# Adds in front of the exponential, and a maximum moved past dense products, in a two-layer transformer kernel

## The chip, the cores and the metric

The kernel runs on one core of one Trainium2 chip. Five engines of the core matter: TensorE multiplies matrices (PE in the profile, PEld for its weight loads), VectorE (DVE), ScalarE (ACT) and GpSimd (POOL) work element by element, and SyncE (SP) issues nearly all DMAs. Each engine takes its own instructions strictly in the order in which they were issued; between engines, semaphores hold an instruction until what it reads is written and what it overwrites is free. The metric is the device time of one execution in microseconds, the median of several runs.

## What is computed

Two layers work on 4 sequences of 1024 tokens with 256 channels. The first layer is a recurrent attention and a mixture of eight experts. The second layer, which holds the change, is an attention over pairs of tokens and a gated feed-forward network with three wide products. The core of the pair attention, per query token i and key token j:

```python
q = einsum('bnc,ac->bna', X, Wq)          # 64 features a
k = einsum('bnc,ac->bna', X, Wk)
e = relu(rho(q[:, :, None, :] + k[:, None, :, :]))   # in effect sqrt(relu(q + k) + eps)
scores = einsum('bija,a->bij', e, Wphi)
m = max(scores, axis=-1)
ex = exp(scores - m)
part1 = einsum('bij,bjc->bic', ex, Vy)
Ew = einsum('bij,bija->bia', ex, e)       # e weighted with ex
out = (part1 + Ew @ We) / sum(ex)
```

The feed-forward network after it is silu(x W1) * (x W2), then two 1024x1024 layers with Gelu, then W3.

## The kernel before

The function `pair_attention` runs the second layer, from 1269 us to the end. It writes out the order of all instructions by hand.

**Blocks, pairs and slots.** There are 128 blocks (class `Block`), each for 32 queries. The 64 features and 32 queries of a block are handled as 16 tiles of 128 partitions x 1024 keys, two to a *pair*, so eight pairs to a block. A pair lives in one buffer `s` of a ring of 14. Its life has four steps:

- `begin` (L1377 ff.) takes a ring buffer and lets POOL do its adds (L1381): the tile number i (0 to 15) in `ADD_ON_POOL`.
- `adds` (L1386) lets VectorE add what neither POOL nor ScalarE has (L1392).
- `pair` (L1396) lets ScalarE add the tiles in `RELU_ON_SCALAR` (L1403), take the square root of the whole pair (L1404), and lets TensorE sum the features into the block's scores `sc` (L1408), eight matmuls that the profile counts as 16.
- `weigh` (L1454), on VectorE, multiplies a tile with the spread exponentials `xb` and sums. After both tiles of a pair the ring buffer is free.

Here an add is relu(key + query), with the query as a per-partition scalar.

**The maximum and the exponential.** When the scores of a block are complete, `top` takes the maximum over a row quarter (L1418), places it in one of four columns (`quarters`, L1420), and a small product with `same` (L1421) brings the four quarters together. `exps` takes the negated maximum (`neg`, L1425, VectorE) and the exponential (`ex`, L1427, ScalarE), and calls `switch`, which runs the dense stream's waiting Silu or Gelu (L1357). The exponential and the root need different activation tables, so a table load stands ahead of each change. `spread` copies the exponentials to all partitions (L1434, TensorE, into `xb`), which the next block's weighings need.

**The main loop** goes over blocks n and slots p = 0 to 7. A slot weighs the two tiles of pair p of block n, with the adds of the pair to be made between them, then issues `work(ROOM[p])`, a counted portion of other work, and then begins one pair and makes one pair that was begun two slots ahead. The pair made in slot p is number 8n + p + 12: pairs 4 to 7 of block n + 1 in slots 0 to 3, pairs 0 to 3 of block n + 2 in slots 4 to 7. So the scores of block n + 1 are complete in slot 3; its maximum comes in slot 5, its exponential in slot 6.

**Other work.** `work` first runs what is due of the dense stream on VectorE (`tick`: the scalings of dense products, L1280 and L1299, two slots after the product), then issues matmuls of the feed-forward network (L1245 for the first products, L1315 for the two wide layers, L1336 for the last) and of the finished blocks (L1505, L1517). One group of dense products takes eight blocks, and it stops at each Silu or Gelu until the next exponential. Lines L913, L922, L926 and L929 are its layer norm.

The places in the loop that the change touches:

```python
cur.weigh(p, 0, ew)
if made < 8 * N:
    blocks[made // 8].adds(made % 8)
cur.weigh(p, 1, ew)
if nxt and p == 5:
    blocks[n + 1].top()
if nxt and p == 6:
    blocks[n + 1].exps()
    blocks[n + 1].spread(0)
work(ROOM[p])
```

Of the kernel before, what the change touches and what calls it, by code (L numbers as in the profile page):

```python
# [8 lines left out]
AF = mybir.ActivationFunctionType  # L9
# [22 lines left out]
PREP = 12  # L32
ROOM = (4, 6, 6, 6, 6, 4, 3, 6)
LATE = 2
RELU_ON_SCALAR = (2, 6, 8, 12, 14)
FIRST_ON_SCALAR = 6
ADD_ON_POOL = (1, 3, 5, 9, 11, 13)
LEAD = 2
# [5 lines left out]
@with_exitstack  # L44
def block_kernel(ctx: ExitStack, tc: tile.TileContext, a, out):
    nc = tc.nc
    keep = ctx.enter_context(tc.tile_pool(name="keep", bufs=1))


    kept = ctx.enter_context(tc.tile_pool(name="kept", bufs=1, space=DRAM))  # L50
    link = {
        "x1": [kept.tile([U, C], F32, tag=f"x1_{j}", name=f"x1_{j}") for j in range(B * T // U)],
        "x2": [kept.tile([FB, C], F32, tag=f"x2_{j}", name=f"x2_{j}") for j in range(B * T // FB)],
        "gates": [kept.tile([1, 2, B, C], F32, tag=f"gates{j}", name=f"gates{j}") for j in range(2)],
        "brow": kept.tile([1, C], F32, tag="brow", name="brow"),
        "yg": kept.tile([P, 4, U], F32, tag="yg", name="yg"),
        "qd": kept.tile([T, 64], F32, tag="qd0", name="qd0"),
        "kd": kept.tile([8, P, T], F32, tag="kd0", name="kd0"),
        "vd": kept.tile([T, C + 1], F32, tag="vd0", name="vd0"),
    }  # L60

    ident = keep.tile([P, P], F32, tag="ident", name="ident")
    nc.scalar.dma_start(ident, a["ident"])
    eps = keep.tile([P, 3], F32, tag="eps", name="eps")
    for i, v in enumerate((EPS_LN, EPS_GN, EPS_RHO)):
        nc.vector.memset(eps[:, i : i + 1], v)
    cols = [keep.tile([P, 6, 2, B], F32, tag=f"mcols{i}", name=f"mcols{i}") for i in range(2)]
    seen = keep.tile([P, NE], F32, tag="seen", name="seen")
    link["qt"] = [keep.tile([P, 64, 8], F32, tag=f"qt{i}", name=f"qt{i}") for i in range(2)]
    nc.gpsimd.memset(seen, 0.0)  # L70
    first_layer(tc, a, link, cols, seen, ident, eps)
    pair_attention(tc, a, link, out, cols, seen, ident, eps)
# [750 lines left out]
def pair_attention(tc, a, link, out, cols_of, seen, ident, eps):  # L823
# [10 lines left out]
    nc = tc.nc  # L834
    NB = T // 32
# [3 lines left out]
    with tc.tile_pool(name="at_k", bufs=1) as pk, tc.tile_pool(name="at_w", bufs=1) as wp, tc.tile_pool(  # L839
# [14 lines left out]
        kB, qtab, kds, vds = {0: {}}, {0: link["qt"][0]}, {0: link["kd"]}, {0: link["vd"]}  # L854
# [18 lines left out]
        for i in range(2):  # L873
            t = wp.tile([P, 4, P], F32, tag=f"ewt{i}", name=f"ewt{i}")
            nc.gpsimd.memset(t, 0.0)
            ewt.append(t)
            t = wp.tile([P, 4, 64], F32, tag=f"ew{i}", name=f"ew{i}")
# [168 lines left out]
        def tick():  # L1046
            for x in late:
                x[0] -= 1
            while late and late[0][0] <= 0:
                late.pop(0)[1]()  # L1050
                banks[0] += 1
# [205 lines left out]
        def follower():  # L1257

            return groups.get(stream[1]) if len(stream) > 1 else None
# [103 lines left out]
        class Block:  # L1363


            def __init__(self, n):
                self.n, self.b, self.s, self.added = n, n // NB, {}, set()
                self.sc = psc.tile([P, 512], F32, tag="sc", name="sc")

            def on_scalar(self, i):  # L1370
                return i in RELU_ON_SCALAR if self.n else i < FIRST_ON_SCALAR

# [3 lines left out]
            def begin(self, p):  # L1376
                self.s[p] = ring.tile([P, 2, T], F32, tag="s", name="s")  # L1377
                for h in range(2):
                    i = 2 * p + h
                    if self.n and i in ADD_ON_POOL:  # L1380
                        nc.gpsimd.tensor_scalar(  # L1381
                            self.s[p][:, h, :], kB[self.b][i % 8], self.query(i), 0.0, ALU.add, ALU.max
                        )

            def adds(self, p):
# [3 lines left out]
                for h in range(2):  # L1389
                    i = 2 * p + h  # L1390
                    if not (self.n and i in ADD_ON_POOL or self.on_scalar(i)):
                        nc.vector.tensor_scalar(  # L1392
                            self.s[p][:, h, :], kB[self.b][i % 8], self.query(i), 0.0, ALU.add, ALU.max
                        )

            def pair(self, p):  # L1396
                t = self.s[p]
                s = p // 4
                self.adds(p)
                for h in range(2):  # L1400
                    i = 2 * p + h
                    if self.on_scalar(i):
                        nc.scalar.activation(t[:, h, :], kB[self.b][i % 8], AF.Relu, bias=self.query(i))  # L1403
                nc.scalar.activation(t, t, AF.Sqrt, bias=eps_rho)  # L1404
                for h in range(2):
                    g = (2 * p + h) % 8
                    for j in range(4):
                        nc.tensor.matmul(  # L1408
                            self.sc[32 * j : 32 * j + 32, 0:256],
                            wsel[:, g, 16 * (1 - s) : 16 * (1 - s) + 32],  # L1410
                            t[:, h, 256 * j : 256 * (j + 1)],
                            start=p == 0 and h == 0,
                            stop=p == 7 and h == 1,
                        )
# [121 lines left out]
        N = B * NB  # L1536
        blocks = {0: Block(0)}
        begun = made = 0
# [3 lines left out]
        def work(room):  # L1542


            tick()
            turns[0] += 1
            if issues and turns[0] % 2:
                issues.pop(0)()
            for of in (tasks, stream):
                while of and room > 0:  # L1550
                    got = next(of[0], self_done)
                    if got is self_done:
                        of.pop(0)
                    elif got is None:
                        break
                    else:
                        room -= got
# [10 lines left out]
        def make():  # L1568
            nonlocal made
            n, p = made // 8, made % 8  # L1570
            if n < N:
                blocks[n].pair(p)
                if n % NB == NB - 1 and n + 1 < N and p >= 4:
                    for g in range(2 * p - 8, 2 * p - 6):
                        spread_keys(n // NB + 1, g)
            made += 1
# [13 lines left out]
        for n in range(N):  # L1590
            cur = blocks.pop(n)
            ew = ews[n // 4 % 2]
            if n % 4 == 0:
                exT = p2.tile([P, 4, 2, P], F32, tag="exT", name="exT")
            nxt = n + 1 < N
            if n % NB == PREP and n // NB + 1 < B:
                stream.insert(min(1 + (follower() in heads), len(stream)), prepare(n // NB + 1))
            for p in range(8):
                if p == 0:
                    cur.spread(1)  # L1600
                    cur.turn()
                if p == 2:
                    cur.turned(exT)
                cur.weigh(p, 0, ew)
                if made < 8 * N:
                    blocks[made // 8].adds(made % 8)
                cur.weigh(p, 1, ew)
                if nxt and p == 5:
                    blocks[n + 1].top()
                if nxt and p == 6:  # L1610
                    blocks[n + 1].exps()
                    blocks[n + 1].spread(0)
                work(ROOM[p])
                while begun <= 8 * n + p + ahead[0]:
                    begin()
                    make()
            if n % 4 == 3:
                tasks.append(finish(n, ew, exT))
# [104 lines left out]
```

## Time and profile before

| what | value |
|---|---|
| median of 3 runs | 5141.64 us (5141.53 to 5143.81) |
| profiled execution | 5137.34 us |
| its span | 5135.6 us, 75609 instructions |
| granted TensorE clock, mean | 0.90 |
| ScalarE roots (L1404) | 1024, 2000 ns each |
| ScalarE adds (L1403) | 641, 1138 ns each |
| VectorE weighings (L1454) | 2048, 1209 ns each |
| VectorE adds (L1392) | 645, 922 ns each |
| POOL adds (L1381) | 762, 3792 ns each |
| exponentials (L1427) | 128, 473 ns each |

A row of a group gives the line of the kernel, the engine, the operation, the tiles written and read, how often, then the busy time and the mean of one, and after the bar the idle time of the engine just before these instructions and which engine's work ended it. A row of a timeline gives start and duration in us. Two instructions that follow each other on VectorE or ScalarE can overlap by about a tenth of a microsecond in such rows, so the distance from start to start is the better price. All times within an execution are counted from the start of its span.

### The profile page before, as it was taken

How to read it: one execution, taken by the hardware profiler on the slowest of the kernel's cores; microseconds unless marked ns; L12 is line 12 of the kernel's file. 1: busy time of each engine (PE TensorE's matmuls, PEld its weight loads, DVE VectorE, ACT ScalarE, POOL GpSimd, SP SyncE). 2: the span in 40 equal slices, each digit the busy share in tenths (PEclk: the TensorE clock that was granted, in tenths of full speed). 3: DMA queues.
4: the chain of work that ended last, by engine and by line, in shares of the span. 5: the costliest groups of instructions: out<-in, count | busy, mean ns of one | idle time of the engine just before them, and what ended most of it. 6: DMA issues, size and time to landing. Idle time of an engine off the chain costs nothing.

```text
span 5135.6 us, 75609 instructions
## 1 busy us (share of the span) xinstructions
PE 4334.1 (84%) x28714; PEld 2437.5 (47%) x28714; DVE 4175.7 (81%) x7255; ACT 3690.1 (72%) x3438; POOL 3396.9 (66%) x1233
## 2 busy tenths in 40 slices
PE   6788888877688979888887988888889889798888
PEld 2233333333234635555554555555455556455557
DVE  5877777765799888888888888888888988988871
ACT  2322222213899889999998889999888999999961
POOL 3533343433688777787887778788867877887840
PEclk8798888988798989999898999999889999999999
DMA  4233333344011222222121323222223222121223
GB/s 137 85 101 105 96 97 89 88 115 117 18 36 58 82 86 87 98 74 83 61 73 51 118 76 111 69 78 71 72 72 108 99 77 80 62 79 66 73 82 114
DMA packets 255787, 429.16 MB, mean 84 GB/s; under 512 B 71752, under 2 KB 142592, under 8 KB 255168
## 3 DMA queue, kind: packets, MB, share of 16 engines
q1 hardware_dynamic: 251776, 420.76, 25.8%
q8 instruction: 227, 3.72, 0.3%
q10 hardware_dynamic: 3168, 1.99, 0.1%
q0 software_dynamic: 480, 1.57, 0.1%
q14 instruction: 136, 1.11, 0.1%
HBM read 396.13 MB, written 40.67 MB: 85 GB/s over the span
## 4 chain that ended last, share of the span: by engine, by line
PE 34%; ACT 18%; DVE 15%; issue 7%; POOL 1%; DMA 0%; ACTq 0%; POOLq 0%; SPq 0%; DVEq 0%
PE ff_ps L1315 14%; PE sc L1408 10%; DVE s L1454 9%; ACT s L1404 9%; ACT s L1403 4%; PE xb L1434 2%; DVE s L1392 2%; PE out_ps L1336 2%; PE o L1505 2%; ACT L1404 2%; ACT L1357 1%; PE o L1517 1%; PE ff_ps L1245 1%; ACT wide L1357 1%; ACT ex L1427 1%
## 5 line engine op out<-in xcount | busy, mean ns | idle before, releaser
L1381 POOL TENSOR_SCALAR s<-kB,qt 128x1024 f32<-128x1024 f32 x762 | 2879.7, 3792 | 603.6 <-DVE ew L1454 480.4
L1454 DVE CUSTOM_DVE_ANT_0 s<-s,xb 128x1024 f32<-128x1024 f32 x2048 | 2417.0, 1209 | 35.1 <-PE xb L1434 33.7
L1404 ACT ACTIVATE s<-s,eps 128x2048 f32<-128x2048 f32 x1024 | 2027.6, 2000 | 76.0 <-DVE s L1392 30.4
L1408 PE MATMUL sc<-s,wsel 128*32 128x256 f32 x16384 | 1198.5, 417 | 404.6 <-ACT s L1404 402.5
L1315 PE MATMUL ff_ps<-wide,fw 128*128 128x256 f32 x4096 | 1006.0, 395 | 29.2 <-ACT wide L1357 25.6
L1408 PEld LDWEIGHTS sc<-s,wsel 128*32 128x32 f32 x16384 | 456.2, 115 | 1006.9 <-ACT s L1404 600.3
L1315 PEld LDWEIGHTS ff_ps<-wide,fw 128*128 128x128 f32 x4096 | 765.7, 194 | 237.6 <-issue 99.5
L1403 ACT ACTIVATE s<-kB,qt 128x1024 f32<-128x1024 f32 x641 | 728.9, 1138 | 23.5 <-DMA yg<-out_g 22.8
L1392 DVE TENSOR_SCALAR s<-kB,qt 128x1024 f32<-128x1024 f32 x645 | 594.1, 922 | 0.4 <-DMA kB<-kd 0.4
L729 POOL TENSOR_TENSOR kv<-vb,out_k 128x512 f32<-128x512 f32 x256 | 323.1, 1270 | 285.5 <-DVE state L797 225.5
L607 PE MATMUL e_ps<-wd,hid 128*128 128x512 f32 x896 | 429.1, 626 | 34.0 <-DVE acc L590 33.2
L1434 PE MATMUL xb<-ex,pick 64*128 64x256 f32 x2048 | 324.9, 440 | 56.9 <-ACT ex L1427 56.9
L797 DVE TENSOR_TENSOR_SCAN state<-dec,carry,kv 128x512 f32<-128x512 f32 x256 | 325.9, 1273 | 9.9 <-POOL carry L792 5.0
L607 PEld LDWEIGHTS e_ps<-wd,hid 128*128 128x128 f32 x896 | 176.0, 202 | 281.0 <-issue 273.4
L1434 PEld LDWEIGHTS xb<-ex,pick 64*128 64x128 f32 x2048 | 195.4, 206 | 194.6 <-ACT ex L1427 96.8
L1245 PE MATMUL ff_ps<-wide,fw 128*128 128x256 f32 x1024 | 266.0, 409 | 6.1 <-ACT wide L929 5.8
L799 DVE TENSOR_TENSOR pr<-state,rec 128x512 f32<-128x512 f32 x256 | 176.0, 687 | 113.2 <-ACT state L795 66.5
L789 ACT COPY carry<-state 128x1 f32<-128x1 f32 x255 | 47.8, 187 | 263.9 <-DVE state L797 262.9
L1245 PEld LDWEIGHTS ff_ps<-wide,fw 128*128 128x128 f32 x1024 | 197.4, 202 | 64.9 <-issue 25.3
L1418 DVE TENSOR_REDUCE sc<-sc 128x1 f32<-128x256 f32 x128 | 54.9, 429 | 208.9 <-PE sc L1408 208.8
L1299 DVE TENSOR_TENSOR wide<-ff_ps,ffn_s 128x512 f32<-128x512 f32 x128 | 87.7, 685 | 167.7 <-PE ff_ps L1315 167.7
L1427 ACT ACTIVATE ex<-sc,neg 128x256 f32<-128x256 f32 x128 | 60.6, 473 | 201.0 <-DVE neg L1425 200.1
(254 smaller groups left out, 4002.8 us busy)
## 6 DMA issues: line engine op xcount, KB each, us to landing
fw<-in_ffw_dram SPq DMA_DIRECT2D x354, 512.0 KB
vb<-vd SPq DMA_DIRECT2D x1024, 64.0 KB
lent<-vd SPq DMA_DIRECT2D x64, 514.0 KB
wd<-in_w_down_dram SPq DMA_DIRECT2D x28, 1024.0 KB
kB<-kd SPq DMA_DIRECT2D x32, 512.0 KB
lent<-in_We_dram SPq DMA_DIRECT2D x32, 512.0 KB
kd<-nd SPq DMA_DIRECT2D x24, 512.0 KB
vd<-out_v SPq DMA_DIRECT2D x8, 512.0 KB
```

The lines of the kernel that those rows point to most:

```text
L607: nc.tensor.matmul(ps, hid[:, k, t * P : (t + 1) * P], wd[:, k, :], start=k == 0, stop=k == HID // P - 1)
L729: nc.gpsimd.tensor_mul(kv, vb[:, g % 2, :], ready[u]["k"][:, n // HN, :])
L797: nc.vector.tensor_tensor_scan(s[:, 1 : U + 1], dec, kv, c, ALU.mult, ALU.add)
L1245: nc.tensor.matmul(ps[:, h, :], w[:, k, o : o + P], hT[:, k, :], start=k == 0, stop=k == 1)
L1315: nc.tensor.matmul(ps[:, h, :], w[:, k * P : (k + 1) * P], of[:, k, :], start=k == 0, stop=k == 7)
L1381: nc.gpsimd.tensor_scalar(self.s[p][:, h, :], kB[self.b][i % 8], self.query(i), 0.0, ALU.add, ALU.max)
L1392: nc.vector.tensor_scalar(self.s[p][:, h, :], kB[self.b][i % 8], self.query(i), 0.0, ALU.add, ALU.max)
L1403: nc.scalar.activation(t[:, h, :], kB[self.b][i % 8], AF.Relu, bias=self.query(i))
L1404: nc.scalar.activation(t, t, AF.Sqrt, bias=eps_rho)
L1408: nc.tensor.matmul(self.sc[32 * j : 32 * j + 32, 0:256], wsel[:, g, 16 * (1 - s) : 16 * (1 - s) + 32], t[:, h, 256 * j : 256 * (j + 1)], s ...
L1434: nc.tensor.matmul(xb[:, 256 * j : 256 * (j + 1)], pick[q, j % 2, s, :], self.ex[q, :], start=True, stop=True)
L1454: nc.vector.tensor_tensor_reduce(t[:, h, :], t[:, h, :], self.xb[s], 1.0, 0.0, ALU.mult, ALU.add, ew[:, self.n % 4, col : col + 1])
```

## The change

Three things are moved; nothing is computed differently. Two of ScalarE's tiles are others (2 and 6 become 4 and 7). In slot 6, ScalarE's adds of the two pairs that are begun and not yet made (pairs 2 and 3 of block n + 2) are issued ahead of the exponential, by a new method `relus` that notes which pairs have had it. In the same slot, `exps` moves from behind the second weighing to between the weighings. In slot 5, `top` moves from ahead of `work` to behind it.

```diff
-RELU_ON_SCALAR = (2, 6, 8, 12, 14)
+RELU_ON_SCALAR = (4, 7, 8, 12, 14)
...
+            def relus(self, p):
+                if p in self.relued:
+                    return
+                self.relued.add(p)
+                for h in range(2):
+                    i = 2 * p + h
+                    if self.on_scalar(i):
+                        nc.scalar.activation(self.s[p][:, h, :], kB[self.b][i % 8], AF.Relu, bias=self.query(i))
+
             def pair(self, p):
                 t = self.s[p]
                 s = p // 4
                 self.adds(p)
-                for h in range(2):
-                    i = 2 * p + h
-                    if self.on_scalar(i):
-                        nc.scalar.activation(t[:, h, :], kB[self.b][i % 8], AF.Relu, bias=self.query(i))
+                self.relus(p)
                 nc.scalar.activation(t, t, AF.Sqrt, bias=eps_rho)
...
                 cur.weigh(p, 0, ew)
                 if made < 8 * N:
                     blocks[made // 8].adds(made % 8)
+                if nxt and p == 6:
+                    for m in range(made, min(begun, 8 * N)):
+                        blocks[m // 8].relus(m % 8)
+                    blocks[n + 1].exps()
                 cur.weigh(p, 1, ew)
+                if nxt and p == 6:
+                    blocks[n + 1].spread(0)
+                work(ROOM[p])
                 if nxt and p == 5:
                     blocks[n + 1].top()
-                if nxt and p == 6:
-                    blocks[n + 1].exps()
-                    blocks[n + 1].spread(0)
-                work(ROOM[p])
```

With these tiles VectorE keeps 0, 2, 6, 10 and 15 instead of 0, 4, 7, 10 and 15; POOL's six are the same.

More of the change, by code (lines that the diff above doesn't have):

```diff
@@ L1366, in __init__ @@
             def __init__(self, n):
-                self.n, self.b, self.s, self.added = n, n // NB, {}, set()
+                self.n, self.b, self.s, self.added, self.relued = n, n // NB, {}, set(), set()
                 self.sc = psc.tile([P, 512], F32, tag="sc", name="sc")
```

## The prediction

> **What bounds the kernel now.** I read the page first, then the last stage (the pair scores, 1269 to 4990 us, 3721 of 5135.6 us), then one repeating stretch of it. Only this stage holds the edited lines.
>
> ```profile
> PE 4334.1 (84%) x28714; PEld 2437.5 (47%) x28714; DVE 4175.7 (81%) x7255; ACT 3690.1 (72%) x3438; POOL 3396.9 (66%) x1233
> ...
> L1418 DVE TENSOR_REDUCE sc<-sc 128x1 f32<-128x256 f32 x128 | 54.9, 429 | 208.9 <-PE sc L1408 208.8
> ...
> L1427 ACT ACTIVATE ex<-sc,neg 128x256 f32<-128x256 f32 x128 | 60.6, 473 | 201.0 <-DVE neg L1425 200.1
> ```
>
> ScalarE waits 200 us at the exponential for the negated maximum, VectorE 209 us at the maximum for TensorE's scores. These are the two places that the change touches.
>
> The starts of the exponential repeat every eight blocks, with the dense products of one group. One such cycle lies between the exponentials at 4229.33 and 4456.71 us: blocks of 31.71, 28.65, 26.33, 29.44, 29.43, 24.71, 30.89 and 26.22 us; I call them A to H. The windows view of it:
>
> ```profile
> 4229.80:4457.20 227.40, 194.83 (x1592) 120.27 (x1584) 200.70 (x357) 208.64 (x156) 184.11 (x52) 0.92 0.20 70
> ```
>
> ScalarE (fourth figure) has 208.6 of 227.4 us to do, VectorE 200.7, TensorE 194.8: none of the three has 15% to spare, and each waits for another in turn. The waits of the same cycle:
>
> ```profile
> ACT ex L1427 <- DVE neg L1425: 11.1, 4, 4.6
> DVE sc L1418 <- PE sc L1408: 9.8, 5, 4.4
> ```
>
> So only four of eight exponentials wait: A 2.07, B 3.95, C 0.47, E 4.64 us. In D, F, G and H ScalarE comes to its exponential after the maximum is there. The timelines of the end of E, of TensorE, then ScalarE, then VectorE (start, duration, idle before):
>
> ```profile
> 4372.36 1.07 PE L1408 MATMUL sc<-s,wsel 128*32 128x256 f32 x16
> 4373.36 0.38 PE L1421 MATMUL sc<-quarters,same 128*128 128x4 f32 x2
> 4373.60 1.97 PE L1315 MATMUL ff_ps<-wide,fw 128*128 128x256 f32 x8
> 4375.50 1.07 PE L1408 MATMUL sc<-s,wsel 128*32 128x256 f32 x16
> 4376.51 1.13 PE L1434 MATMUL xb<-ex,pick 64*128 64x256 f32 x8
> ```
>
> ```profile
> 4368.96 1.28 ACT L1427 ACT_TABLE_LOAD   x1
> 4374.88 0.47 ACT L1427 ACTIVATE ex<-sc,neg 128x256 f32<-128x256 f32 x1 [4.64 <-DVE neg L1425]
> 4375.38 1.28 ACT L1404 ACT_TABLE_LOAD   x1
> ```
>
> ```profile
> 4369.78 0.43 DVE L1418 TENSOR_REDUCE sc<-sc 128x1 f32<-128x256 f32 x1 [2.65 <-PE sc L1408]
> ...
> 4370.92 1.21 DVE L1454 CUSTOM_DVE_ANT_0 s<-s,xb 128x1024 f32<-128x1024 f32 x1
> ...
> 4372.06 1.59 DVE L1392 TENSOR_SCALAR s<-kB,qt 128x1024 f32<-128x1024 f32 x1
> 4373.57 1.20 DVE L1454 CUSTOM_DVE_ANT_0 s<-s,xb 128x1024 f32<-128x1024 f32 x1
> ...
> 4374.70 0.15 DVE L1425 TENSOR_REDUCE neg<-sc 128x1 f32<-128x4 f32 x1
> ```
>
> To be seen: TensorE runs through without idle time; the small product with `same` (L1421) stands ahead of eight records of dense products (1.90 us to the next start); the negation comes two weighings and an add after the maximum, when `same` is long done.
>
> **The change, part by part.** No instruction is added or removed on any engine, no DMA moves, SP's and POOL's orders stay. What moves:
>
> 1. ScalarE's add of tile 2 (pair 1) goes to VectorE, tile 4 (pair 2) from VectorE to ScalarE, 6 and 7 (pair 3) change places. ScalarE's adds of pairs 2 and 3 then stand ahead of the exponential: two of 1.14 us (L1403: 641 in 728.9 us) where one stood, ahead of pair 1's root. The work between two exponentials stays the same, so blocks where ScalarE never waits gain nothing. The roots of pairs 3 to 7 and 0 come one add (1.14) earlier after the exponential.
> 2. VectorE's add of tile 2 now stands between the weighings of slot 5, and pair 1's root waits for it. Behind that root: the two adds, the table load, the exponential.
> 3. The maximum, with `same`, goes behind the dense products of slot 5 on TensorE, and behind the scalings due in that slot on VectorE.
> 4. The negation goes ahead of the second weighing of slot 6, and no add of slot 6 is ahead of it: one weighing (1.14 from start to start) and one add (0.75 to 1.6) less. Whatever holds the negation now holds that weighing, the four instructions after it and the ring slots that they free for POOL.
>
> Block by block, against the exponential's start of before (B and C, and D and E, in one sum each):
>
> A. VectorE's add for pair 0 ends at 4252.43. Then two weighings 2.28, the add of tile 2 at 0.75 to 1.5, root 2.0, two adds 2.3, load 1.28: the exponential at 4261.0 to 4261.7, before 4261.04. 0 to +0.7; I take 0.3, nearer the uncontended add, which is the median row (0.75). The wait of 2.07 is filled, but by work that was elsewhere.
>
> B, C. In B TensorE has no idle time from 4265 on; scores of pair 0 end at 4288.99. Dense products 1.9, `same` 0.39, negation and hand-over 0.2: exponential at 4291.5 instead of 4289.68, +1.8. VectorE reaches the negation about 4287.2 and stands 4 us; its next block starts at 4295.5 instead of 4293.43. C has 1.54 us of waiting for a dense product (at 4306.11) that swallows part; pair 0's add ends 0.55 later, at 4309.6. The chain of A from there, 8.6 to 9.4, gives 4318.2 to 4319.0 instead of 4316.01: +2.2 to +3.0. Lower end +0.9, if B's late exponential alone comes through and half of it is absorbed; I take 2.3, near the sum.
>
> D, E. From C's Gelu on TensorE runs through two blocks (one wait of 0.72 for a root, which now comes earlier). In E `same` moves from 4373.36 to 4375.26, the exponential to 4375.85: +1.0, less 0.72 gives +0.25. I take 0.6. The adds in front hide in E's wait of 4.64. The copy of the exponential through `pick` is due at 4376.51 as before, so TensorE does not wait.
>
> F. ScalarE has no idle time here, so every wait for VectorE is paid. VectorE stands one weighing later against the exponential (1.14), the roots one add earlier (1.14). Root 5 started 1.47 after its add had ended: now it waits 0.8. Root 0 has 1.63 left of which 0.2 stays; tile 2's add follows pair 0's by 3.0 to 3.8, while root 1 could follow root 0 by 1.95: 0.9 to 1.7 more. Together 0 (if VectorE catches up) to 2.5; I take 1.5.
>
> G. VectorE is held by an output product (4.02 us) that hangs on Gelu, so ScalarE's gain of one add is lost again at the layer norm's copy, and both adds then stand ahead of the exponential: 0 to +1.06, taken 0.6. H has 2.8 us of slack before root 0: 0.
>
> Sum 0.3 + 2.3 + 0.6 + 1.5 + 0.6 = 5.3 us a cycle; ends 1.15 and 8.3. There are 16 groups of dense products; the first, and parts of others where keys are prepared, look different, so I count 14 cycles: +74 us (16 to 116). The profiled execution took 5137.34 us (span 5135.6, 1.7 around it), 4.3 below the median of the runs; so about 5141.64 + 74 = 5216.
>
> On the add of tile 2: rows of L1392 run from 0.74 to 1.70 us, median 0.75, though POOL is busy 81% of the cycle. The Trainium skill, page "SBUF — State Buffer", section "Who interferes with whom", says that a VectorE tensor_scalar in a two-port mode and a GpSimd instruction exclude each other for the whole instruction, whoever comes second being fully blocked. If so here, half of a POOL add of 3.7 us would be waited for, about 1.1 more than I took in A, C, F and G: 62 us more, 5278. The rows show no such add, so the measurement decides.
>
> **Rivals.** *Faster: the filled wait is a gain.* The way from exponential to root 7 to maximum is one add shorter and the negation has less ahead of it. If TensorE reaches `same` in time, each of the four waiting exponentials comes 1.14 earlier: 14 x 4 x 1.14 = 64 us, 5078; with A and C alone 5110. For it: 200 us of waiting. Against it: in B, D and E TensorE has nothing but products in its queue. It decides where `same` stands less than 1.14 us behind the negation's earlier place.
>
> *Slower by more:* the late weighings starve POOL. Its adds for pairs 4 to 6 hang on slots 6, 7 and 0; roots 5 and 6 have 3.1 and 2.8 us left in F, of which the change takes 2.3. If these waits come on top, beyond 8.3 a cycle: 5260 to 5290.
>
> *Nothing:* the engines trade waits and each block stays bounded by ScalarE's unchanged work: within 10 us of 5142.
>
> **How the numbers follow.** 0.2% (10 us) is about what a measurement can tell from no change. Slower by the sum (5158 to 5258) 0.56, slower by more 0.11, just above the bound 0.05; nothing 0.08; faster 0.20, half of it below 5105. So slower 0.72, same 0.08, faster 0.20. The time is the sum's 5216; its own range is 5158 to 5258. For 8 in 10 I take 5105 to 5265, leaving out 0.10 on either side.
>
> **What would show it.** Right: idle time of VectorE at the negation, on `same`, near 3 us in B, D and E (9.7 us in all before, then well over 100); ScalarE's wait at the exponential falling from 200 to below 100 us, but its waits for VectorE's adds at the roots (30.4 us) rising to 60 or more; TensorE's wait for `quarters` (76 us) nearly gone; period over 230 us. Wrong: roots 1 and 5 start without waits, or E's and B's exponentials come earlier than before; then the faster rival holds. Should VectorE's stall be there but the period unchanged, ScalarE's work alone bounds, and F and C are mis-sized.

## The result, and the profile after

The changed kernel takes 5229.24 us (median of 4 runs, 5226.91 to 5231.23) against 5141.59 us: 1.0171 times as long, 95% interval 1.0153 to 1.0188. The profiled execution took 5228.88 us with a span of 5227.1, 91.5 us longer than that of before. The forecast was 5216, in a range of 5105 to 5265: the side and the size were right. Which of the moves makes the loss is another matter; one of them, alone, turned out to be a gain.

The page of the changed kernel: the engines, then the share of each engine in the chain that ended last, then rows of the costliest groups (busy time and mean of one, then idle time just before and what ended it). From the line of the root on, lines have moved down by six: the root is L1410, the maximum L1424, `quarters` L1426, the product with `same` L1427, the negation L1431, the exponential L1433, the weighing L1460.

```profile
PE 4375.9 (84%) x28714; PEld 2477.5 (47%) x28714; DVE 4214.1 (81%) x7255; ACT 3686.9 (71%) x3438; POOL 3391.6 (65%) x1233
...
PE 31%; DVE 20%; ACT 18%; issue 5%; POOL 1%; DMA 1%; SPq 0%; ACTq 0%; POOLq 0%; DVEq 0%
...
L1410 ACT ACTIVATE s<-s,eps 128x2048 f32<-128x2048 f32 x1024 | 2021.6, 1999 | 232.8 <-DVE s L1392 190.4
...
L1392 DVE TENSOR_SCALAR s<-kB,qt 128x1024 f32<-128x1024 f32 x645 | 631.9, 980 | 0.1
...
L1431 DVE TENSOR_REDUCE neg<-sc 128x1 f32<-128x4 f32 x128 | 20.4, 159 | 195.4 <-PE sc L1427 195.3
```

The same part of the page for the kernel before, the chain alone:

```profile
PE 34%; ACT 18%; DVE 15%; issue 7%; POOL 1%; DMA 0%; ACTq 0%; POOLq 0%; SPq 0%; DVEq 0%
```

ScalarE is busy for the same time as before (3686.9 against 3690.1 us), VectorE 38 us longer, nearly all of it in its adds, whose mean rose from 922 to 980 ns. VectorE's share of the chain rose from 15 to 20%. Two waits have grown: 190 us at the roots for VectorE's adds (30 before) and 195 us of VectorE at the negation for the product with `same` (10 before). Two others are smaller. The groups of the changed kernel between 1260 and 5100 us, the exponential and the maximum:

```profile
L1433 ACT ACTIVATE ex<-sc,neg 128x256 f32<-128x256 f32 x128 | 60.7, 474 | 104.9 <-DVE neg L1431 103.9
...
L1424 DVE TENSOR_REDUCE sc<-sc 128x1 f32<-128x256 f32 x128 | 54.2, 423 | 65.3 <-PE sc L1414 64.8 <-ACT s L1403 0.4
```

ScalarE's wait at the exponential fell from 200 to 104 us, VectorE's at the maximum from 209 to 65. So the change did fill the waits that it aims at, and the time went up all the same: ScalarE lost 96 us of one wait and gained 160 of another.

The cycle of eight blocks that the prediction worked with (A to H), between the same two exponentials, now takes 235.33 us instead of 227.40. The windows view (stretch, length, then busy time of TensorE, its weight loads, VectorE, ScalarE and POOL, granted clock, share and rate of the DMA engines), and the waits of that stretch (total, times, longest):

```profile
4288.25:4523.58 235.33, 199.27 (x1596) 123.12 (x1596) 204.50 (x355) 208.58 (x155) 183.41 (x51) 0.89 0.20 68
```

```profile
ACT s L1410 <- DVE s L1392: 13.8, 12, 2.3
DVE neg L1431 <- PE sc L1427: 12.8, 5, 4.0
ACT ex L1433 <- DVE neg L1431: 6.1, 3, 4.1
```

ScalarE's busy time is the same to 0.1 us (208.58 and 208.64), so the 7.9 us are idle time of ScalarE. Block by block, exponential to exponential:

| block | A | B | C | D | E | F | G | H | sum |
|---|---|---|---|---|---|---|---|---|---|
| before | 31.71 | 28.65 | 26.33 | 29.44 | 29.43 | 24.71 | 30.89 | 26.22 | 227.38 |
| after | 32.26 | 30.29 | 27.26 | 30.79 | 29.44 | 27.26 | 32.00 | 26.01 | 235.31 |
| difference | +0.55 | +1.64 | +0.93 | +1.35 | +0.01 | +2.55 | +1.11 | -0.21 | +7.93 |

The end of block E in the changed kernel, as timelines of TensorE, ScalarE and VectorE (start, duration, idle before in brackets):

```profile
4431.70 2.86 PE L1315 MATMUL ff_ps<-wide,fw 128*128 128x256 f32 x12
4434.48 1.07 PE L1414 MATMUL sc<-s,wsel 128*32 128x256 f32 x16
4435.49 1.99 PE L1315 MATMUL ff_ps<-wide,fw 128*128 128x256 f32 x8
4437.32 0.28 PE L1427 MATMUL sc<-quarters,same 128*128 128x4 f32 x2
```

```profile
4431.04 2.01 ACT L1410 ACTIVATE s<-s,eps 128x2048 f32<-128x2048 f32 x1 [1.67 <-DVE s L1392]
4432.95 2.17 ACT L1403 ACTIVATE s<-kB,qt 128x1024 f32<-128x1024 f32 x2
4435.14 1.28 ACT L1433 ACT_TABLE_LOAD   x1
4437.83 0.47 ACT L1433 ACTIVATE ex<-sc,neg 128x256 f32<-128x256 f32 x1 [1.41 <-DVE neg L1431]
```

```profile
4429.46 1.48 DVE L1392 TENSOR_SCALAR s<-kB,qt 128x1024 f32<-128x1024 f32 x1
4430.86 1.21 DVE L1460 CUSTOM_DVE_ANT_0 s<-s,xb 128x1024 f32<-128x1024 f32 x1
...
4432.61 0.42 DVE L1424 TENSOR_REDUCE sc<-sc 128x1 f32<-128x256 f32 x1
...
4437.64 0.16 DVE L1431 TENSOR_REDUCE neg<-sc 128x1 f32<-128x4 f32 x1 [3.28 <-PE sc L1427]
4437.72 1.21 DVE L1460 CUSTOM_DVE_ANT_0 s<-s,xb 128x1024 f32<-128x1024 f32 x1
```

All three moves can be read here. VectorE's add of tile 2 (4429.46) takes 1.48 us and ends at 4430.94; the root of pair 1 (4431.04) has waited 1.67 us for it. The two adds in front (4432.95) stand behind that root. Of the 4.64 us that ScalarE waited at the exponential before, 1.41 are left: part of the difference is filled by the adds, and 1.67 of it has only moved to the root. `same` stands behind eight records of dense products, and VectorE stands 3.28 us at the negation, with a weighing behind it.

Summed over the execution: the first ten blocks, in which the wide products do not run yet, became 10.1 us shorter (304.26 to 294.19 from the first exponential to the eleventh). The 116 blocks after them became 98.9 us longer (3367.14 to 3466.03).

The granted clock is lower as well (0.884 against 0.90 in the mean), and what part of the loss is its doing is open. It is not the main part. A record of the wide products (L1315) takes 395 ns in both kernels; among the runs below one with 0.897 is the slowest of all and one with 0.882 is 72 us faster than that; and the new tiles alone, below, lose 1.53% at a mean of 0.898. But over the 46 runs of the kernel before that were taken beside the experiments below, a run with a clock lower by 0.01 was some 25 us longer; taken over to the two kernels, that would be some 35 of the 88 us, an estimate that no run here tests.

### The profile page after: what moved, and what is told of

It reads as the page before. It is cut to its first block, busy times and chain, and to the rows that moved or that the text cites. A ratio compares the mean times of both kernels' runs of the same rounds, so it can differ in the third digit from the quotient of the medians.

```text
span 5227.1 us, 75636 instructions
## 1 busy us (share of the span) xinstructions
PE 4375.9 (84%) x28714; PEld 2477.5 (47%) x28714; DVE 4214.1 (81%) x7255; ACT 3686.9 (71%) x3438; POOL 3391.6 (65%) x1233
## 4 chain that ended last, share of the span: by engine, by line
PE 31%; DVE 20%; ACT 18%; issue 5%; POOL 1%; DMA 1%; SPq 0%; ACTq 0%; POOLq 0%; DVEq 0%
DVE s L1460 13%; PE ff_ps L1315 12%; PE sc L1414 9%; ACT s L1410 7%; DVE s L1392 4%; ACT s L1403 4%; PE out_ps L1336 2%; PE o L1511 2%; PE xb L1440 2%; PE ff_ps L1245 2%; ACT L1433 1%; ACT L1410 1%; ACT wide L1357 1%; ACT L1357 1%; POOL s L1381 1%
## 5 line engine op out<-in xcount | busy, mean ns | idle before, releaser
L1460 DVE CUSTOM_DVE_ANT_0 s<-s,xb 128x1024 f32<-128x1024 f32 x2048 | 2415.6, 1209 | 32.9 <-PE xb L1440 32.8
L1410 ACT ACTIVATE s<-s,eps 128x2048 f32<-128x2048 f32 x1024 | 2021.6, 1999 | 232.8 <-DVE s L1392 190.4
L1414 PE MATMUL sc<-s,wsel 128*32 128x256 f32 x16384 | 1215.5, 423 | 345.8 <-ACT s L1410 341.9
L1315 PE MATMUL ff_ps<-wide,fw 128*128 128x256 f32 x4096 | 1006.7, 395 | 45.7 <-ACT wide L1357 25.2
L1315 PEld LDWEIGHTS ff_ps<-wide,fw 128*128 128x128 f32 x4096 | 765.0, 194 | 271.4 <-issue 110.2
L1403 ACT ACTIVATE s<-kB,qt 128x1024 f32<-128x1024 f32 x641 | 718.1, 1137 | 23.8 <-DMA yg<-out_g 22.8
L1392 DVE TENSOR_SCALAR s<-kB,qt 128x1024 f32<-128x1024 f32 x645 | 631.9, 980 | 0.1
L1431 DVE TENSOR_REDUCE neg<-sc 128x1 f32<-128x4 f32 x128 | 20.4, 159 | 195.4 <-PE sc L1427 195.3
L1336 PE MATMUL out_ps<-fw,wide 128*128 128x256 f32 x512 | 149.4, 446 | 22.8 <-ACT wide L1357 22.8
```

The costliest lines, as they stand in the source:

```text
L1315: nc.tensor.matmul(ps[:, h, :], w[:, k * P : (k + 1) * P], of[:, k, :], start=k == 0, stop=k == 7)
L1392: nc.vector.tensor_scalar(self.s[p][:, h, :], kB[self.b][i % 8], self.query(i), 0.0, ALU.add, ALU.max)
L1403: nc.scalar.activation(self.s[p][:, h, :], kB[self.b][i % 8], AF.Relu, bias=self.query(i))
L1414: nc.tensor.matmul(self.sc[32 * j : 32 * j + 32, 0:256], wsel[:, g, 16 * (1 - s) : 16 * (1 - s) + 32], t[:, h, 256 * j : 256 * (j + 1)], s ...
L1460: nc.vector.tensor_tensor_reduce(t[:, h, :], t[:, h, :], self.xb[s], 1.0, 0.0, ALU.mult, ALU.add, ew[:, self.n % 4, col : col + 1])
```

## The experiments

The theory of the prediction was that `same` behind the products and VectorE's late add together make the loss; its faster rival was that a filled wait is a gain. The change has four parts that can be made alone: the maximum behind the products, the negation between the weighings, the tiles, the adds in front. The first four runs undo or do one part.

**The changed kernel with the maximum ahead of the products again**

```diff
+                if nxt and p == 5:
+                    blocks[n + 1].top()
                 work(ROOM[p])
-                if nxt and p == 5:
-                    blocks[n + 1].top()
```

> The changed kernel with one part undone: the maximum and its small product stand ahead of the dense products of slot 5 again. Theory (two losses: VectorE held at the negation behind dense products, and ScalarE held at the root of pair 1 by VectorE's late add with two adds and the exponential behind it): the hold of VectorE at the negation falls from 195 us to under 40, blocks B and D of the cycle lose nothing any more, but C, F and G keep most of their +0.9, +2.5 and +1.1; about 5160 to 5200 us. Rival 1 (the dense products alone are the loss): not slower than before, 5080 to 5145. Rival 2 (the adds alone are the loss): no change against the changed kernel, about 5225.

Measured: 5204.73 us (5200.58 to 5211.42), 1.0129 [1.0107, 1.0151] of the kernel before. Only 0.42% of the 1.71 came back, 5 us less than the least that the theory gave. VectorE's wait at the negation fell from 195 to 78 us, not below 40, but the roots still waited 172 us for VectorE's adds, and block F still took 27.27 us. So the maximum is the smaller part. The one cycle shown above would mislead here: it takes 230.32 us in this run, 5.0 of its 7.9 us less, but over 14 such cycles 2.5 of 6.75 us come back.

**The kernel before with the maximum behind the products alone**

```diff
                 if nxt and p == 6:
                     blocks[n + 1].exps()
                     blocks[n + 1].spread(0)
                 work(ROOM[p])
+                if nxt and p == 5:
+                    blocks[n + 1].top()
```

(and its call ahead of `work` removed)

> The kernel before with one part done: the maximum and its small product stand behind the dense products of slot 5; tiles, adds and negation as before. Theory of two losses: the negation has two weighings and an add to hide behind, so VectorE is held there some 1.5 to 2.5 us in B, D and E, and B and E's exponentials come up to 1.8 us later; +2 to +4 us a cycle, 5170 to 5200. Rival 1 (dense products alone): 5200 to 5235. Rival 2 (adds alone): 5130 to 5150.

Measured: 5164.52 (5162.28 to 5175.23), 1.0054 [1.0036, 1.0072]: a loss of 0.54%, just below the theory's interval and outside those of both rivals. Block B took 31.61 us instead of 28.65, C gave 1.62 of it back, D lost 0.86. That is the mechanism of the prediction: VectorE waits 2.2 us at the negation in each of B, D and E. Over 14 cycles the loss is 2.1 us a cycle, where the terms of the maximum in the prediction's sum (1.8 in B, 0.6 in D and E) make 2.4.

**The changed kernel without the adds in front**

```diff
                 if nxt and p == 6:
-                    for m in range(made, min(begun, 8 * N)):
-                        blocks[m // 8].relus(m % 8)
                     blocks[n + 1].exps()
```

> The changed kernel without ScalarE's adds ahead of the exponential: tiles 4 and 7 are added when their pairs are made, the maximum stays behind the dense products, the negation between the weighings. Theory of two losses: C and G lose less, since only the table load stands behind the root of pair 1; B, D and E keep theirs; 5180 to 5210. Rival 1: about 5225 as with the change. Rival 2: 5130 to 5150.

Measured: 5276.83 (5267.91 to 5288.44), 1.0269 [1.0239, 1.0299]: slower still, which no theory had. With these tiles the adds in front are a gain of 0.96%. Without them ScalarE waits 281 us at the exponential (104 with them). A, B and E take 1.1 to 1.4 us more each, G and H 1.7 and 2.2, and C and F 2.4 us less. So it is neither the maximum nor the adds in front that make most of the loss; what is left is the set of tiles.

**The kernel before with the negation between the weighings alone**

```diff
+                if nxt and p == 6:
+                    blocks[n + 1].exps()
                 cur.weigh(p, 1, ew)
                 if nxt and p == 5:
                     blocks[n + 1].top()
                 if nxt and p == 6:
-                    blocks[n + 1].exps()
                     blocks[n + 1].spread(0)
```

> The kernel before with one part done: negation and exponential stand between the weighings of slot 6; tiles, adds and maximum as before. Theory of two losses: the small product is done in time, so the negation comes one weighing (1.14 us) earlier in A, C and E, less in B; 1 to 3 us a cycle gained, 5095 to 5130. A rival in which the weighing that is moved behind the negation delays ring buffers, POOL and the roots as much as the exponential gains: 5135 to 5150.

Measured: 5095.95 (5089.72 to 5108.38), 0.9919 [0.9895, 0.9943]: faster than both kernels. ScalarE's wait at the exponential falls from 200 to 148 us and nothing takes its place: the roots wait 35 us for VectorE's adds (30 before), the negation 52 for `same`.

The next four runs test the set of tiles.

**The changed kernel with the old tiles**

```diff
-RELU_ON_SCALAR = (4, 7, 8, 12, 14)
+RELU_ON_SCALAR = (2, 6, 8, 12, 14)
```

> The changed kernel with the old five tiles (2, 6, 8, 12, 14): maximum behind the dense products, negation between the weighings, and of the adds in front of the exponential only tile 6's is left. Theory (the tiles): what the changed kernel loses is VectorE's add of tile 2 in slot 5, for which the root of pair 1 waits. The negation between the weighings alone gave 5096, the maximum behind alone cost 25 us; with the old tiles the sum is 5121, and with up to 20 for the add in front 5100 to 5135. ScalarE's wait at the roots for VectorE's adds falls from 190 to below 60 us. Rival (the moves together): it is the late maximum and the early negation together that hold VectorE, whatever the tiles: 5190 to 5235.

Measured: 5174.25 (5168.35 to 5190.13), 1.0078 [1.0055, 1.0101]. The tiles give back 0.93%, so the rival falls; but the time is 39 us above the theory's upper end. The roots' waits for VectorE's adds are 80 us, not below 60. Most of what the sum had wrong is the add in front, which costs some 33 us in the run after the next; the rest is that the maximum behind the products costs 46 us on top of that run, where it cost 25 alone.

**The kernel before with the new tiles alone**

```diff
-RELU_ON_SCALAR = (2, 6, 8, 12, 14)
+RELU_ON_SCALAR = (4, 7, 8, 12, 14)
```

> The kernel before with the new five tiles (4, 7, 8, 12, 14) alone: no add in front, maximum and negation in their old places. Theory (the tiles): the run without the adds in front took 5277; less 25 for the late maximum, plus 43 for the early negation, gives 5295 as a plain sum; since waits overlap I expect 5210 to 5300, with more than 80 us of waits at the roots for VectorE's adds. Rival: the tiles cost only where VectorE is also held at an early negation; alone they make 5130 to 5175.

Measured: 5217.59 (5205.98 to 5230.31), 1.0153 [1.0125, 1.0181]. One line of constants, with every other order as before, makes nearly the whole loss. The roots wait 89 us for VectorE's adds, 65 us of idle time at pair 1 alone (9.6 before).

**The negation between the weighings, and tile 6's add in front (old tiles, maximum ahead)**: the changed kernel with the old tiles, and the maximum put back as in the first run.

> The kernel before with the negation between the weighings and the add of pair 3 (tile 6) in front of the exponential; old tiles, maximum ahead of the dense products as before. Theory (a filled wait is a gain where no root is made to wait): the kernel with the negation moved alone took 5096 and has 148 us of waits at 53 exponentials left; an add of 1.14 us in front fills at most 53 x 1.14 = 60 of it: 5050 to 5095. Rival: ScalarE gains nothing by order, and the add makes the exponentials that do not wait late: 5100 to 5140.

Measured: 5128.65 (5123.85 to 5135.89), 0.9987 [0.9978, 0.9997], which is 0.68% above the kernel without that add in front. The rival's number, but not its reason: the exponentials do wait less (112 instead of 148 us), and the roots wait more. The rows of the root in the run with the negation alone, and in this one:

```profile
L1404 ACT ACTIVATE s<-s,eps 128x2048 f32<-128x2048 f32 x1016 | 2013.8, 2000 | 81.7 <-DVE s L1392 35.1 <-POOL s L1381 1.3 <-ACT s L1403 0.7
```

```profile
L1410 ACT ACTIVATE s<-s,eps 128x2048 f32<-128x2048 f32 x1019 | 2013.0, 1999 | 116.7 <-DVE s L1392 67.2 <-POOL s L1381 9.9 <-ACT s L1403 0.7
```

The 36 us that the exponentials win are lost again at the roots (35 us). The rest of the loss stands at two other places where ScalarE now comes early: its copy behind the transposes (`exT`, idle time 0.5 to 18 us between the exponentials of blocks 10 and 126) and the layer norm (L913 and L929, 47 to 64 us).

**The changed kernel with VectorE's add of tile 2 one slot earlier**

```diff
                 if made < 8 * N:
                     blocks[made // 8].adds(made % 8)
+                if p == 4 and made + 1 < 8 * N:
+                    blocks[(made + 1) // 8].adds((made + 1) % 8)
```

> The changed kernel with VectorE's add for pair 1 (tile 2) issued one slot earlier, behind that for pair 0 in slot 4. Theory (a late add holds the root): the root of pair 1 no longer waits, the block F of the cycle goes from 27.3 back to about 24.7 us, and the time to 5110 to 5170; the waits of the roots for VectorE's adds fall from 190 to below 90 us. Rival (VectorE has too much to do here): the add is only moved, the weighings of slot 4 and the maximum come later by as much, and the time stays at 5205 to 5245.

Measured: 5162.48 (5159.56 to 5164.82), 1.0050 [1.0035, 1.0065]. One add issued two weighings earlier gives back 1.2 of the 1.7%. Block F takes 25.56 us (27.26 with the late add, 24.71 before), and the roots wait 74 us for VectorE. So with two adds in front, the late add of tile 2 is what makes the new tiles cost. ScalarE in its block F comes to the two adds without a stop:

```profile
4407.19 3.98 ACT L1410 ACTIVATE s<-s,eps 128x2048 f32<-128x2048 f32 x2 [0.30 <-DVE s L1392]
4411.08 2.17 ACT L1403 ACTIVATE s<-kB,qt 128x1024 f32<-128x1024 f32 x2
```

against the changed kernel, where the second of these roots stands alone behind a wait of 1.67 us, and the kernel before, where neither root waits in block F:

```profile
4456.02 2.01 ACT L1410 ACTIVATE s<-s,eps 128x2048 f32<-128x2048 f32 x1 [0.30 <-DVE s L1392]
4459.70 2.00 ACT L1410 ACTIVATE s<-s,eps 128x2048 f32<-128x2048 f32 x1 [1.67 <-DVE s L1392]
4461.61 2.17 ACT L1403 ACTIVATE s<-kB,qt 128x1024 f32<-128x1024 f32 x2
```

```profile
4391.25 3.90 ACT L1404 ACTIVATE s<-s,eps 128x2048 f32<-128x2048 f32 x2
4395.05 1.13 ACT L1403 ACTIVATE s<-kB,qt 128x1024 f32<-128x1024 f32 x1
4396.28 2.00 ACT L1404 ACTIVATE s<-s,eps 128x2048 f32<-128x2048 f32 x1
```

The last four runs ask how many adds of ScalarE should stand in front, and whether a version beats the one with the negation alone.

**The negation between the weighings, new tiles, tile 2 earlier; no adds in front**: the fourth kernel with the tiles (4, 7, 8, 12, 14) and the two lines of the run above.

> The kernel before with the negation between the weighings, the new tiles, and VectorE's add of tile 2 one slot earlier (slot 4); no adds in front, maximum ahead of the dense products. Theory (the new tiles cost only through that late add): as the kernel with the negation moved alone, 5070 to 5105, the waits at the root of pair 1 below 15 us. Rival (two adds of ScalarE behind the exponential instead of one hold the later roots): 5120 to 5160.

Measured: 5159.15 (5153.74 to 5174.44), 1.0042 [1.0029, 1.0056]. The theory falls. The roots are in time (5.6 us at pair 1, less than before), but ScalarE waits 220 us at the exponential. The end of block E shows it, first with the negation moved alone, then here:

```profile
4324.11 1.28 ACT L1427 ACT_TABLE_LOAD   x1
4329.03 0.47 ACT L1427 ACTIVATE ex<-sc,neg 128x256 f32<-128x256 f32 x1 [3.63 <-DVE neg L1425]
```

```profile
4378.48 1.28 ACT L1427 ACT_TABLE_LOAD   x1
4384.55 0.47 ACT L1427 ACTIVATE ex<-sc,neg 128x256 f32<-128x256 f32 x1 [4.78 <-DVE neg L1425]
4384.92 1.14 ACT L1403 ACTIVATE s<-kB,qt 128x1024 f32<-128x1024 f32 x1
```

The wait is longer by 1.15 us, one add of ScalarE (1.14), and that add now stands behind the exponential. With the old tiles, ScalarE's add of tile 2 had filled part of this wait all along. So the new tiles have two prices: the late add at the root of pair 1, and, unless adds are put in front, an add less ahead of the exponential. The rival has the right number for another reason than the one it gave: the later roots wait no more than before.

**The changed kernel with the maximum ahead and tile 2 earlier**

> The changed kernel with the maximum put back ahead of the dense products and VectorE's add of tile 2 one slot earlier. Theory (adds in front make roots 0, 5 and 6 wait for VectorE and POOL, whatever the tiles): the run with the add earlier took 5162, less 25 for the maximum: 5125 to 5145, some 35 above the same kernel without adds in front; roots 0, 5 and 6 wait 70 us together, where they wait 30 without. Rival (the adds in front are a gain as soon as pair 1's add is in time): below 5095, and below the kernel without them.

Measured: 5140.37 (5129.81 to 5147.05), 1.0000 [0.9990, 1.0011], inside the theory's interval. Roots 0, 5 and 6 have 63 us of idle time ahead of them, 27 in the run without adds in front. But the adds in front are a gain of 19 us against that run, not a loss of 35: the theory's price for them was that of the old tiles, where one add stands in front anyway.

**The negation ahead of VectorE's add of slot 6 too (old tiles, nothing else)**: `exps` ahead of `adds` in slot 6 of the fourth kernel.

> The kernel with the negation between the weighings, the negation put ahead of VectorE's add of slot 6 as well; old tiles, nothing else. Theory (only one exponential a cycle, in block A, still comes late by VectorE's order): 0 to 13 us less than 5096, 5080 to 5098. Rival (the negation now stands at the product with `same` in B, D and E for another add's time, and holds add, weighing and POOL): 5105 to 5130.

Measured: 5098.24 (5091.77 to 5102.55), 0.9916 [0.9894, 0.9939], at the theory's upper end: no difference to the negation between the weighings that these runs can tell. In block A the exponential's wait falls from 0.92 to 0.24 us; the idle time at the negation rises from 52 to 98 us over blocks 11 to 126.

**Tile 6's add in front, and all of VectorE's adds one slot earlier**

```diff
-                if made < 8 * N:
-                    blocks[made // 8].adds(made % 8)
+                for m in range(made, min(made + 2, 8 * N)):
+                    blocks[m // 8].adds(m % 8)
```

> The kernel with the negation between the weighings and tile 6's add in front of the exponential (old tiles, maximum ahead; it took 5129, 33 us above the same without the add in front), with all of VectorE's adds issued one slot earlier. Theory (an add in front loses because ScalarE then comes to roots 0, 5 and 6 before VectorE's adds are there): these roots wait below 35 us together instead of 67, and the time falls to 5080 to 5105. Rival (VectorE has no room: adds issued earlier make the weighings, the ring slots and POOL's adds later by as much): 5120 to 5150, with more waiting of POOL for the weighings than the 555 us of that run.

Measured: 5110.48 (5109.94 to 5114.24), 0.9950 [0.9933, 0.9967]: 18 us faster than the same without the move, and 15 slower than the negation alone. Between the two expectations. The row of its roots:

```profile
L1410 ACT ACTIVATE s<-s,eps 128x2048 f32<-128x2048 f32 x1016 | 2000.4, 1998 | 86.7 <-POOL s L1381 46.5 <-DVE s L1392 3.1 <-ACT s L1403 1.1
```

The waits for VectorE's adds are gone (67 to 3 us), as the theory said, and POOL's adds are late next (9.9 to 46.5 us). Roots 0, 5 and 6 together go from 67 to 26 us, and root 1 from 10 to 28. POOL itself waits less for the weighings (501 instead of 555 us), so the rival's reason is not seen.

**Put together.** The moves, stacked one on the other, each step measured:

| kernel | ratio to before | step |
|---|---|---|
| before | 1.0000 | |
| + negation between the weighings | 0.9919 | -0.81% |
| + adds in front, old tiles (tile 6 alone) | 0.9987 | +0.68% |
| + new tiles | 1.0129 | +1.42% |
| + maximum behind the products (the changed kernel) | 1.0171 | +0.42% |

In another order the steps differ; the adds in front are a loss with the old tiles and a gain with the new. A table of ScalarE's idle time explains why. Idle time ahead of each instruction of a kind is summed from the traces, for the exponentials of blocks 11 to 126 and the roots of blocks 12 to 127, in us; the last column is ScalarE's whole idle time between the exponentials of blocks 10 and 126. At the roots the first 20 ns of each gap are left out.

| kernel (adds of ScalarE between root 0 and exponential) | us | exponential | root 0 | root 1 | roots 5 and 6 | all idle |
|---|---|---|---|---|---|---|
| before (1) | 5142 | 176 | 20 | 10 | 9 | 317 |
| negation between (1) | 5096 | 136 | 21 | 10 | 8 | 283 |
| + tile 6 in front (2) | 5129 | 103 | 42 | 10 | 25 | 321 |
| the same, all VectorE adds earlier (2) | 5110 | 109 | 0 | 28 | 26 | 314 |
| negation between, new tiles, tile 2 earlier (0) | 5159 | 200 | 18 | 6 | 9 | 352 |
| + adds in front (2) | 5140 | 110 | 38 | 5 | 25 | 328 |
| changed kernel, tile 2 earlier (2) | 5162 | 136 | 44 | 6 | 38 | 354 |
| new tiles alone (0) | 5218 | 194 | 20 | 65 | 9 | 407 |
| changed kernel, maximum ahead (2) | 5205 | 62 | 39 | 109 | 21 | 385 |
| changed kernel (2) | 5229 | 92 | 43 | 122 | 30 | 420 |

What these 116 blocks take beyond ScalarE's idle time, its busy time, is 3038 to 3054 us in every kernel of this study, so this table is where the time lies. With no add in front the exponential waits too long, with two the roots that follow it come before their adds are there. One add in front is the fastest of what was measured, and with the new tiles the late add of tile 2 comes on top at pair 1.

## Why the prediction was right, point by point

**The sum.** Predicted: 5.3 us a cycle in 14 cycles, 74 us. Measured over the same 14 cycles (blocks 14 to 125): 6.75 us in the mean, 94 us. But that mean hides two kinds. The eight cycles like the one that the prediction read lose 7.9 to 12.7 us, 9.2 in the mean; the six others change by -1.3 to +8.0, 3.5 in the mean. The step "so I count 14 cycles" held by luck: the cycles of the kind that it read were sized too small, and six were not of this kind. The cycle shown is not typical in its single terms either: over the 14 cycles A loses 0.74, B and C together 1.62, D and E 1.59, F 0.93, G 1.20 and H 0.66 us, since in the six others B becomes 0.86 and F 1.23 us shorter and E 1.98 longer.

**A, +0.3 (0 to 0.7).** Measured +0.55 in the cycle shown, and 0.74 in the mean of 14. The mechanism is right, the tile's price was not: I stayed near the median add, 0.75. In slot 5 the add of tile 2 has a mean of 1.21 us and a median of 1.47.

**B and C, +2.3 (0.9 to 3.0).** Measured +1.64 and +0.93, together 2.57. `same` behind the products was sized at +1.8 for B, and in B the negation waits 3.97 us for it, where I had said 4. In the run with the maximum moved alone, B lost 2.96 and C won 1.62 back, which is the absorption that I had left as the lower end.

**D and E, +0.6 (0.25 to 1.0).** Measured +1.35 and +0.01, beyond the upper end. The step "in E `same` moves from 4373.36 to 4375.26, the exponential +1.0" put the loss in the wrong block. `same` also stands behind dense products in D, where the signs expected VectorE to wait near 3 us but the sum gave the exponential no loss: VectorE waits 3.19 us there and the exponential 0.59.

**F, +1.5 (0 to 2.5).** Measured +2.55, the largest term in this cycle. Nearly every part was named: root 5 waits 0.50 us (0.8 predicted), root 1 1.67 (0.9 to 1.7), and the two adds of VectorE stand 3.65 us apart (3.0 to 3.8). Root 0 waits 0.30, where 0.2 of slack was to be left. What failed is the choice between the ends: I allowed VectorE to catch up, and it does not, as it has no idle time in this block at all.

**G, +0.6 (0 to 1.06)**: +1.11 in the cycle shown, 1.20 in the mean of 14. **H, 0**: -0.21 there, but +0.66 in the mean. In this cycle all the terms but B and C were taken too low, D and E, F and G beyond their upper ends; over the 14, B and C and F were taken too high, and the others too low. By moves rather than blocks: the late maximum was sized about right (2.4 us a cycle in the sum, 2.1 alone and 2.5 undone), the late add and what stands behind it too low (the other 2.9 of the sum, while the run that issues the add earlier takes back 4.8 us a cycle), and what the earlier negation gains by itself, 2.3 us a cycle, was not asked.

**The first ten blocks** were said to look different and priced at nothing. They became 10.1 us shorter. Of the parts, the negation alone gives 6.9 of it (297.39), and with tile 6's add in front 10.4 (293.85); the new tiles alone lose 7.0 there (311.28). Where no wide products run, the filled wait is a gain.

**The signs.** VectorE's idle time at the negation: well over 100 predicted, 195 measured. The roots' waits for VectorE's adds: 60 or more, 190 measured. The period over 230: 235.3. The wait at the negation near 3 us in B, D and E: 3.97, 3.19 and 3.28. The wait at the exponential: below 100 predicted, 104 measured, a near miss. TensorE's wait for `quarters` "nearly gone": wrong, it rose from 76 to 126 us (weight loads included). I had thought only of the blocks with dense products in TensorE's queue. The idle time ahead of the product rose where the maximum itself comes later: from 0 to 12.5 us over all blocks F, from 3.0 to 14.6 in G, from 5.7 to 11.3 in C.

**The rule weighed.** The Trainium skill, page "SBUF — State Buffer", section "Who interferes with whom", would have an add of VectorE in a two-port mode wait for the end of a POOL instruction that is under way; the estimate by it was 5278. The add of tile 2 in the changed kernel ran inside POOL's instructions for its whole length in 113 of 117 cases and had a mean of 1.22 us there, against 0.75 for adds beside no POOL work. That is slower than I took, and far from a wait of half a POOL add of 3.8 us. It is 0.47 us above that row, where the estimate by the rule was 1.1 above what I took.

**The rivals.** "A filled wait is a gain" was half right, and its half is a version that beats both kernels: the negation between the weighings, alone, takes 5096 us. The prediction costed the moves only together and never asked what the negation gives by itself. The rest of that rival fell for the reason that the prediction gave in F: ScalarE won at the exponential and lost at the roots. That the late weighings starve POOL is not shown: POOL's wait for weighings rose from 480 to 586 us, but the roots' waits for POOL's adds rose only from 1.3 to 15 us.

## What to carry to other kernels

An add that fills a wait is also an add that was somewhere else: count what stands between the engine's last wait and the next on either side of the move, and ask who has to be earlier for it, since here a second add in front made ScalarE reach the next roots before VectorE and then POOL had fed them. A change of several moves should be costed move by move, for here a gain of 0.8% was buried under one late add that cost 1.2 to 1.3%. What one cycle shows should be checked over many before a part is priced by it. When work passes from one engine to another, it should be issued where the receiving queue still has room ahead of the consumer: for the root of pair 1, two weighings earlier was enough.

## What had not been expected of the hardware

The same VectorE add of 128x1024 takes 0.75 us beside no POOL work, and mostly between 0.74 and 1.5 us beside it, but being beside POOL does not say which. The add of tile 2, over 117 blocks, had a mean of 1213 ns in slot 5 of the changed kernel (70 of 117 above 1.2 us) and 817 ns one slot earlier (11 of 117), though it ran wholly inside POOL's instructions in 113 and in 103 of them. What decides between 0.75 and 1.5 was not found by these runs. Moving the add thus changed its length as well as its place; but the 0.73 us by which the add at 4429.46 exceeds 0.75 are less than half of the 1.67 us that the root waits for it.
